# Row sums moved to ScalarE, the spread of the roots moved three steps on, and four smaller moves in a transformer layer on one core

## The chip, the cores and the metric

The kernel runs on one core of one Trainium2 chip. The metric is the device time of one execution in microseconds (us). Five engines work side by side: TensorE (PE in the profile; its weight loads are PEld), VectorE (DVE), ScalarE (ACT), GpSimd (POOL) and SyncE (SP), which issues most DMAs here. Each engine takes its instructions strictly in the order in which they were laid down for it.

## What is computed

The input x has 4 sequences of 1024 tokens with 256 channels. All numbers are float32. The reference adds two blocks to x, each with a layer norm ahead of it:

```python
x = x + attention(layernorm(x))      # RWKV: 16 heads of 16 channels
x = x + experts(layernorm(x))        # 8 experts, two for each token, at most 320 rows each
...
def layernorm(x):
    m, v = mean(x), var(x)           # over the 256 channels
    return (x - m) / sqrt(v + 1e-5)
...
# attention, per head, in chunks of tokens
att = rc @ kc
yc = att * Wmat @ vc + rc @ state * wb
new_state = ws * state + kc * wk @ vc
# then each head's y is normed, scaled, shifted, multiplied by gelu(xg @ Wg.T), and sent through Wo
...
# experts: softmax and top two of 8 logits, then for each expert on its rows
out = (silu(x @ w1) * (x @ w3)) @ w2
```

## The kernel before: tiles, stages and order

**Tiles.** The 4096 tokens are 16 blocks of 256 tokens (`TB`), four to a sequence. A block is two tiles of 128 tokens. Norms are taken for 512 tokens (`RT` = 4 tiles) at a time, apart from the very first 512 tokens, whose two halves are normed one after the other (`n` = 2).

**One attention block** is made of three generators. Each `yield` in them is a seam at which the order may pass to other work.

- `front` (L350) makes the block's inputs. Its steps are: the normed rows `xn` (ACT); their transposes `trx` on PE, the copy `xT` (ACT) and the shift difference `xx` (POOL, L379); the mix `xm` for the keys (DVE, L385); the keys `pc` on PE (L395) with the copy `kT`; the receptance `rT`, `rbT` and the mix for the gate `xm_g` (POOL); the values `pt` (L432); the transposed keys `pk` (L447) and `kw`; the gate `gT` (gelu on ACT, L458).
- `chunk` (L460), twice for a block: four score products `pa` (L470), multiplied by the decay `wmat` into `aw` (DVE, L478, four of 128x512); later the outputs `y` (L492, L499) and the state's update `pu` (L511) with `upd` (DVE, L518).
- `back` (L532) norms y by heads: squares and a copy on ACT; variances `pv` on PE (L547); a reciprocal root made of small DVE operations in two parts (`rsqrt`, L299: a first guess with one step, then a second step, ending in `ry`, L316); the spread of the roots to all channels `prs` on PE (L562); products `ys` and `zT` on DVE (L569, L570); the output product `po` on PE (L578) and its addition to x (L583).

**Norms.** `norm_stats` (L320) takes a `bn_stats` and a `bn_aggr` for each tile on DVE (L328, L329), then the root in about ten small DVE operations, and the shift `nb` (L336). It is called in three ways: for the two halves of the first 512 tokens, for the attention's next 512 tokens (`st` in the loop, 7 times), and for the experts' norm inside `logits` (8 times).

**Experts.** After 512 tokens are through the attention, `logits` and `route` (L589, L643) compute which experts they go to, and POOL scatters each row to DRAM, to a place of its expert (L783, 8 or 16 scatters). A job is one expert on the rows of one stretch `s`: SP loads weights and rows (`xe`, L831), PE transposes the rows (`pe`, L852), DVE copies them (`xeT`, L858), then come the products `p` (L883), silu on ACT (`sl`), the product `act` on DVE (L872), the results `pw` (L904) and an indirect DMA that adds them to the output (L911). A job of stretch s may begin only when `due(s)` holds: its routing lies at least `LAG` steps back (L948).

**The order of the work.** PE's order is written out by hand (`manual_schedule`, L1052): each block n runs a table of 15 steps (L1067 to L1083), and each step advances some generators. `f` is the front of block n+1, `fa` that of block n+2, `bk` the back of block n-1, `new` that of block n. After each step two seams of the routing are passed (`steps(routing, 2)`), and expert work follows as far as a credit of columns (`RATES`) allows. The other engines' orders are made by a planner, which follows the program's order and its own idea of when inputs are ready. `issue_after` ties an instruction behind another. PSUM has eight banks: tag "m" has four, "f" three and "y" one.

In the table before, `back` is stepped at these places of the next block: `pv` and the first root step at 3, the second root step at 4, `prs` and `zT` at 5, right behind `y` and `pu` of the first chunk, and `po` at 10.

Of the kernel before, what the change touches and what calls it, by code (L numbers as in the profile page):

```python
# [9 lines left out]
F32 = mybir.dt.float32  # L10
I32 = mybir.dt.int32
AF = mybir.ActivationFunctionType
ALU = mybir.AluOpType
# [4 lines left out]
P = 128  # L18
B, T, C = 4, 1024, 256
# [4 lines left out]
TB = 256  # L24
TPB = TB // P
BPS = T // TB
RB = 512
RT = RB // P
# [18 lines left out]
LN_EPS = 1e-5  # L47
# [5 lines left out]

RATES = (470, 1470, 1400, 1400)

LAG = 4

SCORES = (0, 6)
MAGIC = 0x5F3759DF
ROOT = (64.0 / 9.0) ** 2  # L60
# [3 lines left out]
def rwkv_then_moe_kernel(  # L64
# [12 lines left out]
    nc = tc.nc  # L77

    const = ctx.enter_context(tc.tile_pool(name="const", bufs=1))
# [3 lines left out]
    sm = ctx.enter_context(tc.tile_pool(name="sm", bufs=1))  # L83
# [5 lines left out]
    def bank(tag, name):  # L89
        return ps.tile(  # L90
            [P, 512], F32, tag=tag, name=name, bufs={"m": 4, "y": 1, "f": 3}[tag])
# [10 lines left out]
    xb = {}  # L102
# [5 lines left out]
    def load_x(b, r, step=RT):  # L108
        t = keep.tile([P, RT, C], F32, tag="x", name=f"x{b}_{r}", bufs=4)
        src = rows(x, b, r)  # L110
        for i in range(0, RT, step):
            nc.sync.dma_start(out=t[:, i:i + step, :], in_=src[:, i:i + step, :])
        xb[b, r] = t
# [26 lines left out]
    ones = const.tile([P, P], F32, tag="ones", name="ones")  # L140
# [87 lines left out]
    def decay_of_heads(cc):  # L228
        for i in range(cc * HC, (cc + 1) * HC):
            h = order[i]  # L230
            nc.scalar.activation(wmat[:, i, :], dist, AF.Exp, scale=nlam[:, h:h + 1])
# [67 lines left out]
    def rsqrt(v, n, nm):  # L299

        y = sm.tile([P, n], F32, tag=f"ry{n}", name=f"ry{nm}", bufs=2)
        a = sm.tile([P, n], F32, tag=f"ra{n}", name=f"ra{nm}", bufs=2)

        def guess():
            yi, vi, ai = y.bitcast(I32), v.bitcast(I32), a.bitcast(I32)
            nc.vector.tensor_tensor(ai, vi, one_i.to_broadcast([P, n]), ALU.logical_shift_right)
            nc.vector.tensor_tensor(yi, magic_i.to_broadcast([P, n]), ai, ALU.subtract)
            step(1.0)  # L310

        def step(scale):
            nc.vector.scalar_tensor_tensor(a, y, scale, y, ALU.mult, ALU.mult)
            nc.vector.tensor_tensor(a, a, v, ALU.mult)
            nc.vector.scalar_tensor_tensor(a, a, -10.0 / 3.0, a, ALU.add, ALU.mult)
            nc.vector.scalar_tensor_tensor(y, a, 5.0, y, ALU.add, ALU.mult)  # L316

        return y, (guess, lambda: step(9.0 / 64.0))

    def norm_stats(key, src, nm, t0=0, n=RT, behind=None):  # L320

        st = sm.tile([P, n, 6], F32, tag=f"st{n}", name=f"st{nm}", bufs=2)
        mv = sm.tile([P, n, 2], F32, tag=f"mv{n}", name=f"mv{nm}", bufs=2)
        ve = sm.tile([P, n], F32, tag=f"ve{n}", name=f"ve{nm}", bufs=2)
        nb = sm.tile([P, n], F32, tag=f"nb{n}", name=f"nb{nm}", bufs=2)
        for t in range(n):
            with tc.issue_after(behind) if behind else nullcontext():
                nc.vector.bn_stats(st[:, t, :], src[:, t0 + t, :])  # L328
            nc.vector.bn_aggr(mv[:, t, :], st[:, t, :])  # L329
            yield  # L330
        nc.vector.tensor_scalar(ve, mv[:, :, 1], LN_EPS, ROOT, ALU.add, ALU.mult)
        rs, parts = rsqrt(ve, n, nm)
        parts[0]()
        yield
        parts[1]()
        last["nb"] = nc.vector.scalar_tensor_tensor(  # L336
            nb, mv[:, :, 0], -1.0, rs, ALU.mult, ALU.mult).ins
        stats[key] = rs, nb, t0

    stats = {}  # L340

    def normed(dst, src, key, t):
        rs, nb, t0 = stats[key]
        t -= t0
        return nc.scalar.activation(
            dst, src, AF.Identity, bias=nb[:, t:t + 1], scale=rs[:, t:t + 1])

    last = {"base": None, "adds": []}

    def front(b, blk, o):  # L350

        nm = f"{b}_{blk}"
        r, h0 = divmod(blk * TPB, RT)
        src = xb[b, r]
# [9 lines left out]
        xT = a2.tile([P, CC, TB + 1], F32, tag="xT", name=f"xT{nm}")  # L364
# [6 lines left out]
        for cc in range(CC):  # L371
# [4 lines left out]
        last["xT_copy"] = nc.scalar.copy(  # L376
            xT[:, :, 1:TB + 1], pt.rearrange("p (cc i) -> p cc i", cc=CC)).ins
        xx = a1.tile([P, CC, TB], F32, tag="xx", name=f"xx{nm}")
        last["xx"] = last["pool"] = nc.gpsimd.tensor_tensor(  # L379
            xx, xT[:, :, 0:TB], xT[:, :, 1:TB + 1], ALU.subtract).ins  # L380

        def mixed(m):
            xm = a1.tile([P, CC, TB], F32, tag="xm", name=f"xm{nm}_{m}", bufs=3)
# [205 lines left out]
    def logits(b, r):  # L589

        nm = f"{b}_{r}"
        nc.sync.dma_start(out=rows(out, b, r), in_=xb[b, r])
        yield from norm_stats(("f", b, r), xb[b, r], f"f{nm}")
        yield
        hs = a2.tile([P, RT, W], F32, tag="hs", name=f"hs{nm}")
# [346 lines left out]
    clock = Block()  # L942
# [4 lines left out]

    def due(s):  # L948
        g = AFTER[s]
        return g in clock.routed and clock.step >= clock.routed[g] + LAG  # L950

    def flags(e):

# [30 lines left out]
    def routed(b, r):  # L984
        yield from logits(b, r)
        g = segment_of(b, r)
        if (r + 1) * RT == SEGMENTS[g][1] + SEGMENTS[g][2]:
            yield from route(g)
            clock.routed[g] = clock.step

    def steps(gen, n=1):
        for _ in range(n):
            next(gen, None)
# [3 lines left out]
    def fronts(n):  # L997
        if n >= NBLK:
            return iter(()), None
        b, blk = divmod(n, BPS)  # L1000
        o = Block()
        return front(b, blk, o), o
# [3 lines left out]

    for _ in norm_stats(("a", 0, 0, 0), xb[0, 0], "a0_0", 0, TPB):
        pass
    with tc.issue_after(last["nb"]):
        for _ in norm_stats(("a", 0, 0, 1), xb[0, 0], "a0_1", TPB, TPB):  # L1010
            pass
    f, cur = fronts(0)
    steps(f, 4)
    first_xm = last["xm"]
    with tc.issue_after(last["first_xn"]):
        decay_of_heads(0)
    with tc.issue_after(last["xT_copy"]):
# [33 lines left out]
    bk, routing, credit = iter(()), iter(()), 0  # L1051
    with tc.manual_schedule(engines={ENG.PE}):  # L1052
        for n in range(NBLK):
            b, blk = divmod(n, BPS)
            f, (fa, after) = f1, fronts(n + 2)
            st = iter(())
            if n + 2 < NBLK and n % RPS == 0:
                sb, sblk = divmod(n + 2, BPS)
                sr = sblk * TPB // RT
                st = norm_stats(("a", sb, sr, 0), xb[sb, sr], f"a{sb}_{sblk}", behind=last["xm"] if n else first_xm)  # L1060
            if blk % RPS == 0 and b + 1 < B:
                load_x(b + 1, blk // RPS)
            if blk == 0:
                last["state"] = None
            c = [chunk(b, blk, t, cur) for t in range(TPB)]
            new = back(b, blk, cur)
            for i, stage in enumerate((  # L1067
                (c[0], st),
                (f, st),
                (c[0], st),  # L1070
                (bk, st),
                (f, bk, st),
                (c[0], bk, st),
                (c[1], fa, st),
                (f,),
                (fa,),
                (c[1],),
                (bk,),
                (f,),
                (c[1], fa, new),  # L1080
                (f,),
                (bk,),
            )):  # L1083
                for part in stage:
                    steps(part)
                steps(routing, 2)
                clock.step += 1
                credit = min(credit + RATES[clock.turn], 4 * RATES[clock.turn])

                drain = i in SCORES  # L1090
                while credit > 0 or drain:
                    drain = False
                    cols = next(work, None)
                    if cols is None:
                        break
                    credit -= cols
            if n and n * TPB % RT == 0:
                pb, pblk = divmod(n - 1, BPS)
                routing = chain(routing, routed(pb, pblk * TPB // RT))
            cur, nxt, f1, bk = nxt, after, fa, new  # L1100

        clock.mixed = True
        for _ in chain(bk, routing, routed(B - 1, RPS - 1)):
            clock.step += 1
            if clock.step % 2:
                next(work, None)
        clock.mixed = False

        over = sm.tile([P, E + 1], F32, tag="over", name="over")
        nc.vector.tensor_scalar_add(  # L1110
            over[:, :E], last["base"], -float((TILES[B - 1] + SURE) * P))
        nc.vector.tensor_reduce(over[:, E:], last["base"], AX.X, ALU.max)
        nc.vector.tensor_scalar_add(over[:, E:], over[:, E:], -float(TILES[B] * P))
        last["over"] = sm.tile([P, E + 1], I32, tag="overi", name="overi")
        nc.vector.tensor_copy(last["over"], over)
        for _ in work:
            clock.step += 1
# [42 lines left out]
```

## Time and profile before

| | |
|---|---|
| median of 3 runs | 1009.61 us (1008.65 to 1011.55) |
| the profiled execution | 1007.76 us, its span 1006.0 us |
| PE busy | 944.5 us (94%) |
| PEld busy | 751.0 us (75%) |
| DVE busy | 471.6 us (47%) |
| ACT busy | 262.5 us (26%) |
| POOL busy | 247.4 us (25%) |

The span is the time from the first to the last instruction that the profile holds; 1.76 us of the execution's time lie around it. Busy time of an engine is the time that its instructions cover. The profile also cuts the span into 40 slices of 25.15 us with a busy share for each engine; in that table PEclk is the share of full clock that was granted to TensorE. A group of instructions is written as line, engine, operation, what is written and what is read, with the mean duration of one in ns and the idle time ahead of it, put down to whatever ended that idle time.

One product in the code is two MATMUL records in the profile, while a transpose is one: `front` has 3 x 4 key, receptance and gate products in each of 16 blocks, which is 192, and the groups of L395 hold 256 + 128 = 384 records.

### The profile page before, as it was taken

Reading aid. Unit: us, or ns where it says so; the run is one execution under the profiler, and the core shown is the slowest. Engines: PE = TensorE matmul, PEld = TensorE weight load, DVE = VectorE, ACT = ScalarE, POOL = GpSimd, SP = SyncE. Lnnn points to the kernel's source line nnn. Section 1 sums busy time; section 2 is a strip of 40 time slices with the busy share of each in tenths; the row PEclk is TensorE's granted clock in tenths of the full one; section 3 lists DMA queues with packets and bytes.
Section 4 is the critical chain, followed back from the end, with each engine's and each line's share of the span. In section 5 each row is a group of like instructions: output and inputs, shape, how many; then the busy total and the mean of one; then the engine's idle time right before and its main releaser. Section 6 shows DMA issues by size and latency. Waiting matters only on the chain. (4 is left out here: it accounts for less than half of the span.)

```text
span 1006.0 us, 16923 instructions
## 1 busy us (share of the span) xinstructions
PE 944.5 (94%) x6718; PEld 751.0 (75%) x6718; DVE 471.6 (47%) x1436; ACT 262.5 (26%) x559; POOL 247.4 (25%) x268
## 2 busy tenths in 40 slices
PE   5889889999999799999999899999999999999996
PEld 3666677878777678888888777888876866867764
DVE  7888746856677444454544344522222221222221
ACT  5324334244433323132221311311110111111110
POOL 6212410511125501212144111172111111211111
PEclk9999879999999999999999999999999999999998
DMA  5993133444424623334455445576654145423421
GB/s 171 273 302 129 49 129 97 168 131 134 161 88 156 202 79 127 101 114 128 132 164 169 140 117 163 153 222 212 178 164 119 39 142 147 127 56 123 148 53 19
DMA packets 92072, 139.05 MB, mean 138 GB/s; under 512 B 5456, under 2 KB 73552, under 8 KB 91984
## 3 DMA queue, kind: packets, MB, share of 16 engines
q1 hardware_dynamic: 79120, 120.36, 37.0%
q0 software_dynamic: 12720, 17.47, 9.1%
q8 instruction: 58, 0.95, 0.4%
q14 instruction: 30, 0.25, 0.1%
q10 hardware_dynamic: 144, 0.02, 0.0%
HBM read 103.45 MB, written 34.39 MB: 137 GB/s over the span
## 5 line engine op out<-in xcount | busy, mean ns | idle before, releaser
L883 PE MATMUL p<-xeT,w 128*128 128x256 f32 (+2 forms) x1960 | 436.2, 378 | 5.2 <-DVE xeT L858 3.9
L883 PEld LDWEIGHTS p<-xeT,w 128*128 128x128 f32 x1960 | 332.6, 195 | 95.3 <-issue 8.4
L872 DVE TENSOR_TENSOR act<-sl,p 128x256 f32<-128x256 f32 (+2 forms) x245 | 99.5, 408 | 281.9 <-ACT sl L888 166.0
L888 ACT ACTIVATE sl<-p 128x256 f32<-128x256 f32 (+2 forms) x245 | 91.0, 374 | 477.4 <-PE p L883 450.7
L904 PE MATMUL pw<-w,act 128*128 128x256 f32 x938 | 211.2, 381 | 0.5 <-DVE act L872 0.4
L911 POOL DMA_INDIRECT y_out<-ye,xe x67 | 104.6, 1561 | 434.9 <-DVE ye L908 358.5
L904 PEld LDWEIGHTS pw<-w,act 128*128 128x128 f32 x938 | 175.2, 190 | 25.8 <-issue 1.5
L908 DVE TENSOR_SCALAR ye<-pw,xe 128x256 f32<-128x256 f32 x67 | 32.1, 483 | 128.9 <-PE pw L904 128.9
L478 DVE TENSOR_TENSOR aw<-pa,wmat 128x512 f32<-128x512 f32 x128 | 79.4, 684 | 11.3 <-PE pa L470 11.1
L395 PE MATMUL pc<-xm,wa 128*128 128x256 f32 x256 | 66.8, 408 | 5.5 <-DVE xm L385 4.2
L783 POOL DMA_INDIRECT disp<-hs,is x64 | 63.7, 996 | 29.9 <-issue 15.9
L395 PEld LDWEIGHTS pc<-xm,wa 128*128 128x128 f32 x256 | 50.2, 204 | 16.8 <-DVE xm L385 5.8
L385 DVE SCALAR_TENSOR_TENSOR xm<-xx,ch,xT 128x256 f32<-128x256 f32 x96 | 43.9, 487 | 39.1 <-POOL xx L379 32.1
L470 PE MATMUL pa<-rT,kT 32*128 32x256 f32 x512 | 42.0, 412 | 4.1 <-ACT gT L458 3.4
L529 POOL TENSOR_TENSOR state<-state,upd 128x64 f32<-128x64 f32 x24 | 9.1, 377 | 139.5 <-DVE upd L518 125.7
L499 PE MATMUL y<-aw,vpad 128*32 128x128 f32 x1024 | 40.8, 278 | 0.2 <-DVE aw L478 0.2
L470 PEld LDWEIGHTS pa<-rT,kT 32*128 32x128 f32 x512 | 25.6, 188 | 14.3 <-ACT gT L458 5.0
L499 PEld LDWEIGHTS y<-aw,vpad 128*32 128x32 f32 x1024 | 24.5, 109 | 12.9 <-issue 11.3
L422 POOL TENSOR_TENSOR xm_g<-xx,ch 128x512 f32<-128x512 f32 x16 | 17.9, 1119 | 63.6 <-PE pc L395 63.5
L432 PE MATMUL pt<-wa,xm 128*128 128x256 f32 x128 | 32.3, 397 | 0.0
L395 PE MATMUL pc<-xm_g,wa 128*128 128x256 f32 x128 | 31.1, 385 | 0.3 <-POOL empty L1028 0.3
L578 PE MATMUL po<-wa,zT 128*128 128x256 f32 x128 | 30.3, 379 | 0.0
(174 smaller groups left out, 763.3 us busy)
## 6 DMA issues: line engine op xcount, KB each, us to landing
w<-w_in SPq DMA_DIRECT2D x96, 896.0 KB, 6.5
disp<-empty SPq DMA_DIRECT2D x8, 795.0 KB, 13.9
disp<-empty SPq DMA_DIRECT2D x16, 265.0 KB, 8.0
xe<-disp SPq DMA_DIRECT2D x16, 265.0 KB, 2.8
xe<-disp SPq DMA_DIRECT2D x8, 530.0 KB, 3.8
y_out<-x SPq DMA_DIRECT2D x8, 512.0 KB, 3.5
x<-x_in SPq DMA_DIRECT2D x7, 512.0 KB, 4.0
wa<-w_attn_in SPq DMA_DIRECT2D x5, 256.0 KB, 5.3
```

Source lines behind the costliest of these rows:

```text
L385: last["xm"] = nc.vector.scalar_tensor_tensor(xm[:, cc, :], xx[:, cc, :], maa(m, cc), xT[:, cc, 1:TB + 1], ALU.mult, ALU.add,).ins
L395: nc.tensor.matmul(pp[:, m * TB:(m + 1) * TB], wa[w][:, cc, m * P:(m + 1) * P], xm[:, cc, :], start=cc == 0, stop=cc == CC - 1,)
L432: nc.tensor.matmul(pv[:, t * C:(t + 1) * C], xm_v[:, cc, t * P:(t + 1) * P], wa[W_V][:, cc, :], start=cc == 0, stop=cc == CC - 1,)
L470: nc.tensor.matmul(pa[g][:, cc * TB:(cc + 1) * TB], o.kT[rows32, cc, cols], o.rT[rows32, cc, :, cols], start=True, stop=True, tile_positio ...
L478: nc.vector.tensor_tensor(w.rearrange("p q i -> p (q i)"), pa[g], wmat[:, 4 * g:4 * g + 4, :].rearrange("p q i -> p (q i)"), ALU.mult,)
L499: nc.tensor.matmul(y[32 * g:32 * g + 32, :], o.vp[:, t, cc * 4 + g, q * 32:(q + 1) * 32], aw[g][:, cc * 2 + q, :], start=state is None and ...
L783: ins = nc.gpsimd.indirect_dma_start(out=disp[:, :], out_offset=bass.IndirectOffsetOnAxis(ap=idx_s[g][:, c, t:t + 1], axis=0), in_=last["h ...
L872: nc.vector.tensor_tensor(act, sl, p3[:, :w], ALU.mult)
L883: nc.tensor.matmul(pp[:, :w], wt[:, cc, f * P:(f + 1) * P], xeT[:, cc, lo:lo + w], start=cc == 0, stop=cc == CC - 1,)
L888: nc.scalar.activation(sl, p1[:, :w], AF.Silu)
L904: nc.tensor.matmul(po[:, :C], acts[f][:, i * P:(i + 1) * P], w2e[:, f, :], start=f == 0, stop=f == FC - 1,)
L911: ins = nc.gpsimd.indirect_dma_start(out=out[:, :], out_offset=bass.IndirectOffsetOnAxis(ap=xe.bitcast(I32)[:, t, C:C + 1], axis=0), in_=y ...
```

## The change

1. `norm_stats` with four tiles takes the sums on ScalarE: a Copy scaled by -1/256 with an accumulator (minus the mean), then a Square with that mean as bias and an accumulator (256 times the variance). With two tiles it stays on VectorE. 15 calls of four tiles are changed.
2. `prs` and `zT` move from step 5 to step 8, `po` from 10 to 11, and the transposed keys `pk` from 11 to 10.
3. PE runs 20 products of a 128x128 tile of ones ahead of everything; nothing reads their result.
4. The shift difference `xx` of the very first block is taken by VectorE and no longer by GpSimd.
5. `LAG` = 4 for all stretches becomes `LAGS` = (8, 5, 4, 4).
6. The second half of the first 512 tokens' norm is traced after the first four steps of the first front, with its last root step behind the first mix products.

```diff
-LAG = 4
+LAGS = (8, 5, 4, 4)
+WARM = 20
...
     def norm_stats(key, src, nm, t0=0, n=RT, behind=None):
-        for t in range(n):
-            with tc.issue_after(behind) if behind else nullcontext():
-                nc.vector.bn_stats(st[:, t, :], src[:, t0 + t, :])
-            nc.vector.bn_aggr(mv[:, t, :], st[:, t, :])
-            yield
-        nc.vector.tensor_scalar(ve, mv[:, :, 1], LN_EPS, ROOT, ALU.add, ALU.mult)
+        if n < RT:
...
+        else:
+            mean, sign = sm.tile([P, n], F32, tag="mn", name=f"mn{nm}", bufs=2), 1.0
+            for t in range(n):
+                with tc.issue_after(behind) if behind else nullcontext():
+                    nc.scalar.activation(
+                        aside, src[:, t0 + t, :], AF.Copy, scale=-1.0 / C,
+                        accum_out=mean[:, t:t + 1])
+                nc.scalar.activation(
+                    aside, src[:, t0 + t, :], AF.Square, bias=mean[:, t:t + 1],
+                    accum_out=ve[:, t:t + 1])
+                yield
+            nc.vector.tensor_scalar(ve, ve, ROOT / C, LN_EPS * ROOT, ALU.mult, ALU.add)
...
-        last["xx"] = last["pool"] = nc.gpsimd.tensor_tensor(
-            xx, xT[:, :, 0:TB], xT[:, :, 1:TB + 1], ALU.subtract).ins
+        if b == 0 and blk == 0:
+            nc.vector.tensor_tensor(xx, xT[:, :, 0:TB], xT[:, :, 1:TB + 1], ALU.subtract)
+        else:
+            last["pool"] = nc.gpsimd.tensor_tensor(
+                xx, xT[:, :, 0:TB], xT[:, :, 1:TB + 1], ALU.subtract).ins
...
-        return g in clock.routed and clock.step >= clock.routed[g] + LAG
+        return g in clock.routed and clock.step >= clock.routed[g] + LAGS[s]
...
-    with tc.issue_after(last["nb"]):
-        for _ in norm_stats(("a", 0, 0, 1), xb[0, 0], "a0_1", TPB, TPB):
-            pass
+    first_nb = last["nb"]
+
+    warm = bank("f", "warm")
+    for _ in range(WARM):
+        nc.tensor.matmul(warm[:, :P], ones, ones, start=True, stop=True)
     f, cur = fronts(0)
     steps(f, 4)
     first_xm = last["xm"]
+
+    second = norm_stats(("a", 0, 0, 1), xb[0, 0], "a0_1", TPB, TPB)
+    with tc.issue_after(first_nb):
+        steps(second, TPB + 1)
+    with tc.issue_after(first_xm):
+        steps(second)
...
                 (bk, st),
                 (f, bk, st),
-                (c[0], bk, st),
+                (c[0], st),
                 (c[1], fa, st),
                 (f,),
-                (fa,),
+                (fa, bk),
                 (c[1],),
+                (f,),
                 (bk,),
-                (f,),
                 (c[1], fa, new),
                 (f,),
-                (bk,),
+                (),
```

More of the change, by code (lines that the diff above doesn't have):

```diff
@@ L320, in norm_stats @@
     def norm_stats(key, src, nm, t0=0, n=RT, behind=None):
-        st = sm.tile([P, n, 6], F32, tag=f"st{n}", name=f"st{nm}", bufs=2)
-        mv = sm.tile([P, n, 2], F32, tag=f"mv{n}", name=f"mv{nm}", bufs=2)
         ve = sm.tile([P, n], F32, tag=f"ve{n}", name=f"ve{nm}", bufs=2)
         nb = sm.tile([P, n], F32, tag=f"nb{n}", name=f"nb{nm}", bufs=2)
-        for t in range(n):
-            with tc.issue_after(behind) if behind else nullcontext():
+        if n < RT:
+            st = sm.tile([P, n, 6], F32, tag="st", name=f"st{nm}", bufs=2)
+            mv = sm.tile([P, n, 2], F32, tag="mv", name=f"mv{nm}", bufs=2)
+            for t in range(n):
                 nc.vector.bn_stats(st[:, t, :], src[:, t0 + t, :])
-            nc.vector.bn_aggr(mv[:, t, :], st[:, t, :])
-            yield
-        nc.vector.tensor_scalar(ve, mv[:, :, 1], LN_EPS, ROOT, ALU.add, ALU.mult)
+                nc.vector.bn_aggr(mv[:, t, :], st[:, t, :])
+                yield
+            mean, sign = mv[:, :, 0], -1.0
+            nc.vector.tensor_scalar(ve, mv[:, :, 1], LN_EPS, ROOT, ALU.add, ALU.mult)
+        else:
+            mean, sign = sm.tile([P, n], F32, tag="mn", name=f"mn{nm}", bufs=2), 1.0
+            for t in range(n):
+                with tc.issue_after(behind) if behind else nullcontext():
[5 more added lines that the diff above has]
+                    accum_out=ve[:, t:t + 1])
+                yield
+            nc.vector.tensor_scalar(ve, ve, ROOT / C, LN_EPS * ROOT, ALU.mult, ALU.add)
         rs, parts = rsqrt(ve, n, nm)
@@ L336, in norm_stats @@
         last["nb"] = nc.vector.scalar_tensor_tensor(
-            nb, mv[:, :, 0], -1.0, rs, ALU.mult, ALU.mult).ins
+            nb, mean, sign, rs, ALU.mult, ALU.mult).ins
         stats[key] = rs, nb, t0
     stats = {}
+    aside = const.tile([P, C], F32, tag="aside", name="aside")
     def normed(dst, src, key, t):
```

## The prediction

> **What bounds the kernel now.** I read the page's slices first, then the stages, then what PE waited for in each, then the two longest waits in order of time.
>
> ```profile
> PE   5889889999999799999999899999999999999996
> DVE  7888746856677444454544344522222221222221
> PEclk9999879999999999999999999999999999999998
> ```
>
> PE is full from slice 15 (377 us) on, so nothing is to be had there. It is not full in the first 100 to 150 us, and DVE is as busy as PE there. The stages (busy us and instructions of PE, PEld, DVE, ACT, POOL, granted clock, DMA share, GB/s):
>
> ```profile
> 0.00:26.80 26.80, 13.92 (x60) 9.82 (x60) 20.04 (x74) 15.05 (x38) 16.83 (x39) 1.00 0.57 176
> 26.80:113.80 87.00, 74.70 (x941) 55.65 (x942) 76.21 (x259) 31.39 (x62) 20.77 (x28) 1.00 0.73 201
> 113.80:137.30 23.50, 18.23 (x143) 14.97 (x144) 11.13 (x35) 8.10 (x18) 8.19 (x11) 0.65 0.23 75
> 137.30:355.00 217.70, 203.62 (x2000) 168.25 (x2000) 141.14 (x473) 83.92 (x172) 65.04 (x75) 0.98 0.44 143
> ```
>
> From 26.8 to 113.8 us DVE (76.2) is busier than PE (74.7), with ACT at 31.4: the four blocks without expert work are bound by DVE. What PE waited for from 26.8 to 137.3 us (total, times, longest):
>
> ```profile
> PE prs L562 <- DVE upd L518: 6.3, 3, 2.9
> PE pe L852 <- DMA xe<-disp: 4.8, 1, 4.8
> PE prs L562 <- DVE ryh L316: 4.3, 1, 4.3
> PE pc L395 <- DVE xm L385: 1.8, 1, 1.8
> PE trx L373 <- ACT xn L345: 1.1, 2, 0.9
> ```
>
> The root's spread waits once in each of blocks 1 to 4: 6.3 + 4.3 = 10.6 us. PE's timeline around the two longest waits (start, length, line, what, idle ahead):
>
> ```profile
> 109.16 0.31 PE L511 MATMUL pu<-vpad,kw 128*32 128x32 f32 x16
> 113.80 1.23 PE L562 MATMUL prs<-ryh,spread 64*128 64x128 f32 x8 [4.34 <-DVE ryh L316]
> 114.96 2.09 PE L470 MATMUL pa<-rT,kT 32*128 32x256 f32 x16
> ...
> 124.83 0.31 PE L511 MATMUL pu<-vpad,kw 128*32 128x32 f32 x16
> 129.89 0.69 PE L852 MATMUL pe<-ident,xe 128*128 128x128 f32 x2 [4.75 <-DMA xe<-disp]
> 131.09 6.78 PE L883 MATMUL p<-xeT,w 128*128 128x128 f32 x32 [0.52 <-DVE xeT L858]
> ```
>
> Each is paid twice: scores `pa` take 2.09 us after the first wait where they take 1.15 elsewhere. The granted clock is 0.50 from 113.4 to 120.2 (PE busy 6.4 us, half of it lost: 3.2) and from 127.1 to 137.3 (busy 6.9, lost 3.4).
>
> **The parts of the change.**
>
> *a. Start.* 20 products are 40 records. The first 16 records of `pc` take 6.76 us at 12.03, the next such 16 take 3.72 at 26.80: the start runs at half clock, which the clock column does not show. Cold, a record of 128 columns is half of 6.76/16, so 0.21 us, and 40 take 8.5 us; warm from halfway, some 6.5. `ones` is ready at 1.15 and the first transposes start at 8.28, so they cost from nothing to 1.4 us. The gain is up to 3.0 us on `pc`. `xx` on DVE is not in the trace; the nearest rows for 512 columns are a copy at 0.60 and a subtraction at 0.68 against 1.04 on POOL, so 0.4 us earlier. But DVE runs without a break from 11.5 to 24 us (mixes, centred values, nine and seven diagonals), and `xx` (0.68) and the second norm's last five operations (1.0) are put into it. PE's next wait, 1.79 at 26.80, is for the second block's `xx`, which POOL starts at 25.19 behind memsets and selects, and POOL's `xm_g` ahead of those waits for `pc`. I take 2 us; ends: 1.5 lost, 4.3 won.
>
> *b. Blocks 0 to 3.* Off DVE go, per tile:
>
> ```profile
> L328 DVE BATCH_NORM_STATS2 sta<-x 128x6 f32<-128x256 f32 x32 | 12.7, 415 | 2.8 <-DMA x<-x_in 2.8
> L329 DVE BATCH_NORM_AGGREGATE mva<-sta 128x2 f32<-128x6 f32 x32 | 5.3, 173 | 0.0
> L345 ACT ACTIVATE xn<-x,nba,rya 128x256 f32<-128x256 f32 x32 | 18.2, 602 | 25.7 <-DVE nba L336 25.7
> L437 ACT COPY vpad<-pt 128x256 f32<-128x256 f32 x32 | 10.3, 374 | 54.9 <-PE pt L432 54.9
> ```
>
> That is 0.59 us, for 60 tiles 35 us in all; from 26.8 to 113.8, 18 tiles or 10.3 us by the same two rows. ACT gets two operations per tile. Accumulating ones are not in the trace; the nearest rows of 256 columns are 0.37 and 0.60, so 0.75 to 1.2 us, in all 45 to 72 us, and double if each accumulator costs another short instruction (0.2, as a copy of 2 columns). ACT has 262 busy of 1006 and 31 of 87 in this stage; that idle time hides it. Uncovered, a norm is 4 x 1.2 = 4.8 us ahead of `kT` or `gT` in ACT's queue.
>
> The Trainium skill speaks against this: ScalarE: Activation LUTs, Rules for kernel authors, gives adds and multiplies to VectorE. The rows agree per tile (0.59 on DVE, 0.75 or more on ACT); by that alone the 60 tiles would cost 10 us or more, but only if ACT were the late engine, which no wait of this stage shows. Its section What ACT_TABLE_LOAD costs would give, as an estimate, 0.40 for the Copy and 0.49 for the Square.
>
> The spread moved to step 8 has the second chunk's `pa` (1.15), `pt` (1.9) and `trx` (0.6) ahead of it, 3.6 us more cover than the waits of 1.41, 2.92 and 1.95 in blocks 1 to 3 need. With 0.95 at `trx` in block 0, whose norm leaves DVE, 7.2 us go. What is late next is `po`: it needs `zT`, which ends 1.54 us after the spread (two `ys`, two `zT`, 71.38 to 72.92), and at step 11 only `pk` (0.60) lies between. That is 1.0 us in each of three blocks. If the four `aw` (2.48) stand ahead of `ys` on DVE it is 3.5. Net 4.2 won; ends: 7.2 won, 3.2 lost.
>
> *c. Block 4 and the first job.* From the routing's count on PE (ended 106.05) to `pe` (129.89) 23.8 us pass. The chain: DVE to the row numbers 4.5; scatters on POOL, 8 x 1.27, with `xx` (1.04) and a state step (0.3), 13.3 with its 1.54 wait for PE's late `trx`, so 11.5 without it; landing and load, 5.6. That is 21.6 without the wait. PE's own work in the stretch is 12.8 at full clock. `LAGS[0]` puts four steps more ahead of `pe`: 13 (`pc` 1.9), 14 (nothing), 0 (`pa` 1.15) and 1 (`pc` 1.9), 4.9 in all. So 17.7 plus 1.0 for `po` stand against 21.6: a wait of 2.9 stays, with one half-clock stretch (1.7 lost for 3.4). Won: 23.8 - 21.6 + 4.9 = 7.2, and 1.7 of clock: 8.9. Ends: the chain stays at 23.8, 4.9; all is covered, 11.0 + 3.4 = 14.4.
>
> *d. From 137 us on.* Waits at `prs` come to 1.0 + 0.7 + 0.8. Expert work at steps 8 to 10 covers `zT` there. The wait at 343.5 for stretch 1 (3.5 us) has one step more, step 2, which holds no PE work: nothing. Waits of `pa` for `gT` (3.4) may grow with ACT's load, those for `aw` shrink with DVE's. I take 1 us; ends: 6 won, 5 lost. Later stretches only pass work from one time to another.
>
> **Sum.** 2 + 4.2 + 8.9 + 1 = 16.1 us. The profiled execution took 1007.76, so 991.7; it lies 1.85 under the median of the runs, so a median of 993.5.
>
> **Rivals.**
>
> 1. *PE only runs into the next wait.* DVE's relief lets PE reach `pe` sooner, the chain stays at 23.8 and the half clock as it was (c gives 4.9), and `po` waits its full 3.5 in blocks 1 to 3 (b gives -3.2). Sum 2 + 4.9 - 3.2 + 1 = 4.7: 1005. For it: one wait in the traces is always followed by the next one. Against: the `po` group had no idle time ahead of it so far. Chance 0.15, with anything from 1000 to 1006.5.
> 2. *Slower: `po` takes over the wait.* Place: step 11 of blocks 1 to 4, where no expert work lies between `prs` and `po`. If DVE runs as late there as it did at 113.80 (4.3 us), `po` waits 0.95 + 4.3 = 5.2, four times 21, with a half-clock stretch each (4 x 1.7 = 7). Against the 2 + 7.2 + 8.9 won, that is +10: a median of 1020. It decides from a lag of some 3.6 us. For it: root, `aw` and mixes still share DVE. Against: 10.3 us leave DVE. Chance 0.10.
> 3. *ACT becomes the late engine.* One us behind ACT's queue for each of the 15 norms eats the gain: 1008, no change. Chance 0.05.
> 4. *The clock falls again before the first `pc`.* PE idles 2.4 us between `trx` and `pc`. At 127.1 the clock fell 2.0 us into a wait that began at 125.13. Then a gives nothing: 995.5. The Trainium skill, TensorE: Matmul & The Clock Gate, Part 1, lets it fall only after an idle window of 3.4 us, by which the warming would hold; the trace's 2.0 us is against it. Chance 0.15, inside the forecast's range.
> 5. *More than the sum*: the lighter DVE also shortens the 13.5 us of waits from 137 to 355. 980. Chance 0.10.
>
> **Numbers.** The forecast, without or with 4, has 0.60 (985 to 1000); rival 1 has 0.15, 2 0.10, 3 0.05, 5 0.10. A measurement here can tell 0.3% (3 us) from no change. Faster: 0.60 + 0.15 + 0.10 = 0.85; same 0.05; slower 0.10. The range takes in rivals 1 and most of 5 and the ends of a to c: 981 to 1007.
>
> **What would show it.** Right: no idle time ahead of `prs` before 114 us, no half clock there, `po` waits of about 1 us, a wait at the first `pe` under 4 us, ACT near 320 to 340 busy, DVE near 437. Wrong: `po` waits of over 3 us, `pa` waiting for `gT` in every block, or transposes that start after 10 us.

## The result and the profile after

The changed kernel took 996.66 us (median of 4 runs, 996.37 to 998.01) against 1009.13 (1007.96 to 1011.55): a ratio of 0.987 [0.9842, 0.9898], 12.5 us less where 16.1 were forecast, and 3.2 us from the predicted median. Its profiled execution took 998.01, the longest of the four, with a span of 996.3: 9.75 less than the profiled execution before, which with 1007.76 was shorter than each of the four runs of its kernel. All step sizes below are of these two executions, so they add up to 9.8 and not to 12.5.

The page's slices (25 us each now) of the kernel after:

```profile
PE   7999899999999899999999998999999999999995
DVE  7888766676576543544543434422222222222221
ACT  5637445644654423243413222311110111101110
PEclk9999989999999999999999998999999999999998
```

PE is fuller in the first ten slices. The clock column still dips in the slice at 125 us and once more at 600. DVE looks no lighter. The same stages as before (busy us of PE, PEld, DVE, ACT, POOL, then clock, DMA share, GB/s):

```profile
0.00:26.80 26.80, 19.51 (x102) 16.42 (x103) 20.38 (x76) 15.94 (x45) 15.85 (x38) 0.94 0.67 208
26.80:113.80 87.00, 80.50 (x982) 59.24 (x981) 76.22 (x231) 50.99 (x135) 23.69 (x31) 1.00 0.70 196
113.80:137.30 23.50, 20.26 (x167) 15.42 (x167) 13.70 (x50) 13.28 (x39) 7.30 (x10) 0.85 0.25 80
137.30:355.00 217.70, 207.06 (x2084) 168.85 (x2083) 136.92 (x432) 107.00 (x269) 62.80 (x74) 0.99 0.43 141
```

In the second row PE went from 74.70 to 80.50 and ACT from 31.39 to 50.99, but DVE, which the prediction wanted relieved, is at 76.22 after 76.21: the blocks pass faster (982 records of PE instead of 941), and more of DVE's other work falls into the same 87 us. PE's waits from 26.8 to 137.3 us:

```profile
PE po L599 <- DVE zT L591: 2.7, 2, 1.6
PE pa L491 <- ACT gT L479: 2.4, 1, 2.4
PE pt L453 <- DVE rbT L436: 1.2, 1, 1.2
PE po L599 <- ACT xn L363: 1.0, 1, 1.0
```

`prs` and `pe` are gone from this list; `po` came in (three waits, 3.7 us), and `pa`, `pt`. PE's timeline around block 4 and the first job:

```profile
110.47 0.93 PE L583 MATMUL prs<-ryh,spread 64*128 64x128 f32 x8
111.33 0.66 PE L468 MATMUL pk<-ident,kT 128*128 128x128 f32 x4
113.63 1.97 PE L599 MATMUL po<-wa,zT 128*128 128x256 f32 x8 [1.64 <-DVE zT L591]
...
119.42 1.34 PE L491 MATMUL pa<-rT,kT 32*128 32x256 f32 x6
123.19 2.07 PE L491 MATMUL pa<-rT,kT 32*128 32x256 f32 x10 [2.43 <-ACT gT L479]
125.55 3.78 PE L416 MATMUL pc<-xm,wa 128*128 128x256 f32 x8 [0.29 <-DVE aw L499]
129.12 0.63 PE L873 MATMUL pe<-ident,xe 128*128 128x128 f32 x2
```

The spread runs without a wait, its product `po` waits 1.64, and `pe` finds its tokens there. But the scores wait 2.43 for the gate `gT`, and the mix products behind them take 3.78 where they take 1.99 at full clock: from 123.1 to 130.0 the clock is 0.51 with PE busy 6.27, 3.1 us lost. The scores do not read `gT`. By the code they are written into the four PSUM banks of tag "m", and the gate's product holds one of these until the gelu has read it.

Why `gT` was late stands in ACT's timeline of the same kernel:

```profile
119.52 0.42 ACT L340 ACTIVATE aside<-x 128x256 f32<-128x256 f32 x1 [7.18 <-DVE x L604]
119.84 0.19 ACT L340 ACTIVATION_READ_ACCUMULATOR aside<-x 128x1 f32 x1
...
120.57 0.58 ACT L558 ACTIVATE sq<-y 128x512 f32<-128x512 f32 x1
...
122.56 0.57 ACT L479 ACTIVATE gT<-pc 128x512 f32<-128x512 f32 x1
```

The norm's first Copy stood at the head of ACT's queue for 7.18 us, waiting for `x` with `po` added (DVE, L604). The squares `sq` and the gate were behind it, and three more sums came ahead of the gate.

Where the time went can be followed in PE's timelines, since from the 21st expert job on both kernels run the same order:

| point on PE | before | after | gained |
|---|---|---|---|
| first `pc` of the second block (block 1) | 26.80 | 26.40 | 0.4 |
| block 3's second `y` | 98.84 | 96.48 | 2.4 |
| first job's `pe` | 129.89 | 129.12 | 0.8, and 4.5 of step work more ahead of it |
| second job's `pe` | 145.12 | 141.10 | 4.0, and 4.1 of step work more ahead of it |
| 21st job's `pe` | 660.45 | 650.68 | 9.8 |
| last job's `pe` | 958.11 | 948.34 | 9.8 |

Blocks are counted from 0, as in the prediction. The step work comes from `LAGS[0]` and is added up from the start of one row to the start of the next: for the first job the products `pc`, `pa` and `pc` of the steps that go ahead of it (1.73 + 1.08 + 1.73; the prediction had 4.9 from lengths of rows, which overlap), for the second a `pv`, a `pc` and a group of `y` and `pu` (0.36 + 1.73 + 1.98).

### The profile page after: what moved, and what is told of

Read it like the earlier page. It is cut to its first block, busy times and chain, and to the rows that moved or that the text cites. A ratio compares the mean times of both kernels' runs of the same rounds, so it can differ in the third digit from the quotient of the medians.

```text
span 996.3 us, 17100 instructions
## 1 busy us (share of the span) xinstructions
PE 950.4 (95%) x6758; PEld 752.5 (76%) x6758; DVE 458.1 (46%) x1317; ACT 319.4 (32%) x797; POOL 246.5 (25%) x267
## 5 line engine op out<-in xcount | busy, mean ns | idle before, releaser
L904 PE MATMUL p<-xeT,w 128*128 128x256 f32 (+2 forms) x1960 | 431.8, 374 | 5.0 <-DVE xeT L879 3.8
L904 PEld LDWEIGHTS p<-xeT,w 128*128 128x128 f32 x1960 | 327.2, 191 | 95.1 <-issue 9.2
L925 PE MATMUL pw<-w,act 128*128 128x256 f32 x938 | 214.4, 384 | 1.2 <-DVE act L893 1.1
L416 PE MATMUL pc<-xm,wa 128*128 128x256 f32 x256 | 63.7, 394 | 3.2 <-DVE xm L406 1.9
L416 PEld LDWEIGHTS pc<-xm,wa 128*128 128x128 f32 x256 | 47.8, 194 | 13.9 <-DVE xm L406 3.5
L491 PE MATMUL pa<-rT,kT 32*128 32x256 f32 x512 | 44.2, 410 | 6.2 <-ACT gT L479 5.9
L340 ACT ACTIVATE aside<-x 128x256 f32<-128x256 f32 x60 | 24.9, 415 | 51.8 <-DVE x L604 51.0
```

The source lines that it names most:

```text
L416: nc.tensor.matmul(pp[:, m * TB:(m + 1) * TB], wa[w][:, cc, m * P:(m + 1) * P], xm[:, cc, :], start=cc == 0, stop=cc == CC - 1,)
L491: nc.tensor.matmul(pa[g][:, cc * TB:(cc + 1) * TB], o.kT[rows32, cc, cols], o.rT[rows32, cc, :, cols], start=True, stop=True, tile_positio ...
L904: nc.tensor.matmul(pp[:, :w], wt[:, cc, f * P:(f + 1) * P], xeT[:, cc, lo:lo + w], start=cc == 0, stop=cc == CC - 1,)
L925: nc.tensor.matmul(po[:, :C], acts[f][:, i * P:(i + 1) * P], w2e[:, f, :], start=f == 0, stop=f == FC - 1,)
```

## The experiments

Two theories stood against each other. **Order**: the gain is the new table, since `prs` has other products ahead of it while the root is computed. **Relief**: the gain is the 10.3 us that leave DVE. The first four runs undo or do one of the two (before: 1014.9 us on their chip).

**One half at a time.** Undone sums (not shown: buffers of their own for four tiles, and the tie `behind` for `bn_stats`):

```diff
-        if n < RT:
+        if n <= RT:
...
```

> The changed kernel with all norm sums back on VectorE (bn_stats and bn_aggr); everything else stays changed. Theory 'relief': the waits at the root's spread came from VectorE's load, so the 35 us of sums come back to it and most of the gain goes: 1004 to 1008 us, with the po waits of blocks 1, 2 and 4 (1.0, 1.1, 1.6 us) growing to 2 to 4 us each. Theory 'order': the waits came from where the table put the spread, the sums on ScalarE are worth little and even cost the 2.4 us wait of the scores for gT at 120.8 us with the half clock behind it: 993 to 998 us, and that wait is gone.

Measured: 1001.78 us, 0.9889 [0.9851, 0.9927]. The wait of the scores for `gT` is gone from 26.8 to 137.3 us: the gelu, at 123.17, waits only for its product (0.94 us). The waits at `po` did not grow as relief had it (3.3 us in three waits, 3.7 in the change).

Undone table:

```diff
-                (c[0], st),
+                (c[0], bk, st),
...
-                (fa, bk),
+                (fa,),
...
-                (f,),
                 (bk,),
+                (f,),
...
-                (),
+                (bk,),
```

> The changed kernel with the table of steps of before (spread at step 5, po at 10, pk at 11); everything else stays changed. Theory 'relief': VectorE, lighter by 35 us, has the roots ready, the waits at the spread stay small (under 1 us each in blocks 1 to 4): 995 to 999 us. Theory 'order': the spread waits again in blocks 1 to 4, 1.4 to 4.3 us each as before, and po waits are gone: 1002 to 1007 us.

Measured: 1011.58 us, 0.9973 [0.9952, 0.9994]. The old waits are back, from 26.8 to 137.3 us:

```profile
PE prs L583 <- DVE upd L539: 6.4, 3, 3.3
...
PE prs L583 <- DVE ryh L318: 3.1, 1, 3.1
```

Only the sums (the kernel before with the `else` branch of `norm_stats` from the diff):

> The kernel before with only the norm sums of four tiles moved to ScalarE. Theory 'relief': most of the gain comes with it: 998 to 1003 us, waits at the spread from 10.6 us down to under 4 in blocks 1 to 4. Theory 'order': 1006 to 1010 us, waits at the spread stay near 10 us.

Measured: 1013.77 us, 0.9996 [0.9974, 1.0019]. Its stage of blocks 0 to 3, and its waits from 26.8 to 137.3 us:

```profile
26.80:113.80 87.00, 79.19 (x941) 58.73 (x941) 70.45 (x215) 47.68 (x127) 18.58 (x27) 0.94 0.78 200
```

```profile
PE prs L578 <- DVE upd L534: 6.6, 3, 3.3
PE pe L868 <- DMA xe<-disp: 5.1, 1, 5.1
PE prs L578 <- DVE ryh L316: 3.1, 1, 3.1
```

DVE was relieved here (76.21 to 70.45, ACT 31.39 to 47.68), and `prs` still waits 9.7 us of the former 10.6. The same 941 records of PE took 79.19 us here and 74.70 before, since the clock fell twice in this execution (0.94 in the mean); the ratio, from 12 runs, does not rest on that.

Only the table (the kernel before with the table's rows of the diff):

> The kernel before with only the new table of steps (spread at 8, po at 11, pk at 10). Theory 'relief': VectorE is as late as before, so the wait moves to po, 2 to 5 us in each of blocks 1 to 4: 1006 to 1012 us. Theory 'order': the 10.6 us at the spread go, po waits 1 us each: 1000 to 1004 us.

Measured: 1001.06 us, 0.9875 [0.9845, 0.9905], with no wait at `prs` and, from 26.8 to 137.3 us:

```profile
PE pe L852 <- DMA xe<-disp: 5.1, 1, 5.1
PE trx L373 <- ACT xn L345: 2.3, 4, 1.5
...
PE po L578 <- DVE zT L570: 1.4, 1, 1.4
PE po L578 <- issue: 1.3, 2, 1.0
```

All four agree. With the table and without the sums the gain is 1.1 and 1.2%; with the sums and without the table it is 0.3% (beside start and lag) and nothing. **Order holds, and relief falls.** The table's three moves (`prs` with `zT`, `po`, `pk`) were not undone one by one; two runs further down shift the first and the second. What relief overlooked stands in DVE's timeline of the kernel before, ahead of the longest wait at `prs`:

```profile
104.79 0.18 DVE L329 BATCH_NORM_AGGREGATE mvf<-stf 128x2 f32<-128x6 f32 x1
104.88 2.46 DVE L478 TENSOR_TENSOR aw<-pa,wmat 128x512 f32<-128x512 f32 x4
...
108.93 0.28 DVE L552 TENSOR_SCALAR var<-pv 128x128 f32<-128x128 f32 x1
...
111.58 0.29 DVE L316 SCALAR_TENSOR_TENSOR ryh<-rah,ryh 128x128 f32<-128x128 f32 x1
111.79 0.68 DVE L415 TENSOR_TENSOR rbT<-pc,wb 128x512 f32<-128x512 f32 x1
...
113.37 0.29 DVE L316 SCALAR_TENSOR_TENSOR ryh<-rah,ryh 128x128 f32<-128x128 f32 x1
```

The last operation of a norm's sums ends at 104.97. From `var` at 108.93 to the end of the root at 113.66 there are 4.7 us of root steps, each needing the one before it, with routing steps and `rbT` among them, and no `bn_stats` at all. What left DVE had not stood in this wait. At most it had stood ahead of the chain: the four `aw` start 1.1 us after the scores `pa` end (103.76 to 104.88). In `only_sums` this wait is 1.27 shorter (3.07), and those in blocks 1 to 3 are not (6.6 against 6.3).

**The start alone** (the kernel before with the warm products, the first `xx` on DVE and the second norm later):

```diff
+    warm = bank("f", "warm")
+    for _ in range(WARM):
+        nc.tensor.matmul(warm[:, :P], ones, ones, start=True, stop=True)
...
+        if b == 0 and blk == 0:
+            nc.vector.tensor_tensor(xx, xT[:, :, 0:TB], xT[:, :, 1:TB + 1], ALU.subtract)
...
```

> The kernel before with the three edits of the start alone: 20 unused products, the first shift on VectorE, the second half's norm traced later. Prediction's term a: 2 us faster, a ratio of 0.998. Theory 'VectorE's queue': what PE gains at the first products it loses where it next waits for VectorE (centred value weights, mixes of the second block), and the clock falls there: between 1 us faster and 2 us slower, a ratio of 0.999 to 1.002.

Measured: 1009.49 us, 1.0005 [0.9987, 1.0024]: nothing. In this execution the clock fell in the 1.92 us ahead of the first `pc`, whose 16 records took 5.33; and the second block's wait grew from 1.79 to 3.67:

```profile
27.41 3.81 PE L399 MATMUL pc<-xm,wa 128*128 128x256 f32 x10 [3.67 <-DVE xm L389]
```

**The lag alone**, undone and done:

```diff
-LAGS = (8, 5, 4, 4)
+LAGS = (4, 4, 4, 4)
```

> The changed kernel with four steps ahead of every stretch's turn again (8, 5, 4, 4 back to 4, 4, 4, 4). Theory 'cover': the four steps more hold 4.9 us of PE work that covers the rows of the first job; without them PE waits 4 to 7 us at the first pe and the clock falls there: 4 to 6 us slower than the changed kernel, a ratio to before of 0.991 to 0.993. Theory 'moved': with the steps the wait only turned into the one of the scores for gT (2.4 us) with the same half clock, so undoing it changes less than 2 us: a ratio of 0.986 to 0.989.

Measured: 1000.27 us, 0.9915 [0.9889, 0.9941], with the wait back:

```profile
PE pe L873 <- DMA xe<-disp: 5.2, 1, 5.2
```

Here the loads are issued at 120.8 (before: 126.1), and the first `pe` runs at 122.92, 7.0 us earlier than before with the same work ahead of it. Of these, 2.3 us were there when the routing's count began on PE (103.26, before 105.52).

> The kernel before with the new table of steps and the new LAGS, nothing else. The table alone gave a ratio of 0.9875 with a 5.1 us wait at the first pe. Theory 'cover': that wait goes, 4 to 7 us more: a ratio of 0.981 to 0.984, better than the whole change. Theory 'moved': another wait takes its place: 0.986 to 0.989.

Measured (the kernel before with the table and `LAGS`): 997.7 us, 0.9894 [0.9868, 0.992], beside 0.9875 [0.9845, 0.9905] for the table alone. The wait at `pe` is gone, and `pc` waits 2.28 for `aw` at 122 us in its place. The lag's own worth is not shown: its three pairs (0.987 or 0.9881 against 0.9915; 0.9894 against 0.9875; 0.9831 against 0.9824 below) differ in sign, and all their intervals overlap.

**The gate ahead of the norm.** To take away the 2.43 us at `pa`, the experts' norm was put behind the gate in ACT's queue:

```diff
-        nc.scalar.activation(o.gT, channel_major(W_G, xm_g), AF.Gelu)
+        last["gT"] = nc.scalar.activation(o.gT, channel_major(W_G, xm_g), AF.Gelu).ins
...
-        yield from norm_stats(("f", b, r), xb[b, r], f"f{nm}")
+        yield from norm_stats(("f", b, r), xb[b, r], f"f{nm}", behind=last["gT"])
```

> The changed kernel, with the sums of the experts' norms queued behind the gate's gelu on ScalarE (so that gT no longer stands behind a sum that waits for x). Theory 'blocked queue': the 2.4 us wait of the scores for gT near 120 us and the half clock after it (some 3 us) go, and the other waits for gT (3.5 us from 137 to 355) shrink: 3 to 6 us faster than the changed kernel, a ratio of 0.981 to 0.984. Theory 'chain': x itself is late, the wait passes to the norm's end and to hs: under 1 us, a ratio of 0.986 to 0.988.

Measured: 1002.09 us, 0.9933 [0.9907, 0.9959]: a miss, outside both theories and 5.4 us longer than the change's 996.66 (0.987). The waits for `gT` did go (none up to 137.3 us, 0.5 after it up to 355), and others came. PE's waits, from 137.3 to 355 us and, in the second fence, from 26.8 to 137.3:

```profile
PE trh L637 <- ACT hs L363: 4.5, 4, 2.6
```

```profile
PE plt L658 <- ACT lgT L655: 2.9, 1, 2.9
```

The norm itself is now late, and with it `hs`, its transposes and the routing's logits. Here the wait at `gT` was the price of the experts' norm being early.

**The cover of `po`.** The prediction named `po` as late next. Here `po` goes one step on, behind the scan's `y` and `pu` (the kernel before with the table and this):

```diff
-                (bk,),
-                (c[1], fa, new),
+                (),
+                (c[1], bk, fa, new),
```

> The kernel before with the new table, but the output product po one step later still, at step 12 behind y and pu of the second chunk. With the new table alone PE waited for zT at po 1.0 to 1.5 us in blocks 1, 2 and 4 and 2.2 us at 221 us. Theory 'order' (a wait is the cover that the table lacks): y and pu put 1.9 us more ahead, the po waits go, 3 to 6 us faster than the table alone, a ratio of 0.981 to 0.985. Theory 'passed on': x is added later, and the next norm and y wait for it or for kw: within 2 us of the table alone, 0.986 to 0.990.

Measured: **991.71 us**, 0.9824 [0.9797, 0.9852], as expected; the interval just overlaps that of the table alone, 0.9875 [0.9845, 0.9905], on another chip. From 26.8 to 137.3 us `po` waits no more, and `pe` still does:

```profile
PE pe L852 <- DMA xe<-disp: 6.1, 1, 6.1
PE trx L373 <- ACT xn L345: 2.8, 4, 1.5
```

The change itself, run again beside it on the same chip:

> The changed kernel once more, beside these three on one chip: a ratio of 0.984 to 0.990 if it is worth what the table alone is.

Measured: 997.77 us (995.27 to 1000.89), 0.9881 [0.9852, 0.9909]. `po_later` ran from 990.88 to 994.04, below every run of the change, and it has neither the sums on ACT nor the start nor `LAGS`. No version of this study has a lower median. With `LAGS` as well:

> As po_later, with LAGS (8, 5, 4, 4) too. Theory 'order': both waits go, po's and the 5 us at the first pe: a ratio of 0.977 to 0.983, the fastest of all. Theory 'passed on': 0.986 to 0.990.

Measured: 992.2 us, 0.9831 [0.9804, 0.9858], no different from `po_later` and just outside what order gave. The 6.1 at `pe` is gone, and this came in its place, from 26.8 to 137.3 us:

```profile
PE pc L395 <- DVE aw L478: 2.8, 1, 2.8
```

**How far the spread has to move** (the kernel before with the table, but `prs` and `zT` at step 7):

```diff
-                (f,),
-                (fa, bk),
+                (f, bk),
+                (fa,),
```

> The kernel before with the new table, but the spread and zT one step earlier, at step 7 behind the values pt, po still at 11. The spread then has 3.05 us more cover than in the table before, po has trx (0.6) and pk (0.6) ahead of it. Theory 'order': waits at the spread stay under 0.5 us in blocks 1 to 3 and about 1.3 in block 4 (4.34 less 3.05), po waits shrink by 0.6 each: within 2 us of the table alone, a ratio of 0.984 to 0.989. Theory 'relief' (VectorE is late as a whole): the spread waits 1.5 us or more in each block: 0.990 to 0.995.

Measured: 997.29 us, 0.9865 [0.9835, 0.9895]. Blocks 1 to 3 have no wait at `prs` and block 4 one of 1.4, as expected; `po` was expected to wait less and waits 3.5:

```profile
PE po L578 <- DVE zT L570: 3.5, 2, 1.8
...
PE prs L562 <- ACT xn L345: 1.4, 1, 1.4
```

So step 7 is as good as step 8 as far as these runs can tell: the root's delay needs the second chunk's `pa` and `pt`, and hardly the step after them.

## Why the prediction was right, and where it was wrong

| term | predicted | measured | from |
|---|---|---|---|
| a start | 2 | 0.4 | second block's first `pc` |
| b blocks 0 to 3 | 4.2 | 2.0 | block 3's second `y`, 2.4 less 0.4 |
| c block 4, first job | 8.9 | 5.7 | second job's `pe`, 4.0 + 4.1 less 2.4 |
| d the rest | 1 | 1.7 | 9.8 less the others |
| sum | 16.1 | 9.8 | |

The direction and the place held, and the median within 3.2 us: the waits at `prs` went, `po` came next with about 1 us a block, and most of the gain is made before 150 us. Three terms were too large, and one reason was wrong.

**a was mis-sized.** The part that was worked out came: the first `pc` takes 3.72 instead of 6.76, and the warm products delay nothing that shows. But the time was not kept. The lines of the start:

```profile
1.20 7.52 PE L1034 MATMUL warm<-ones 128*128 128x128 f32 x40 [1.20 <-POOL ones L143]
...
11.36 3.72 PE L416 MATMUL pc<-xm,wa 128*128 128x256 f32 x16 [1.92 <-DVE xm L406]
17.91 3.38 PE L453 MATMUL pt<-wa,xm 128*128 128x256 f32 x8 [2.83 <-DVE wa L206]
```

The chunk's next product, `pt`, waits 2.83 us for the centred weights, which stand in DVE's queue behind the mixes, and then runs at half clock (0.50 from 17.3 to 20.7; 3.38 instead of 1.89). In `change_again` and `only_start` it went the other way: the clock fell ahead of the first `pc` (5.41 and 5.33), and PE waited 3.59 and 3.67 at the second block's `pc`, which began at 27.42 and 27.41, 0.6 later than before. Its mixes need `xx` from POOL, and there POOL starts it at 25.81 and 25.80, behind its memsets and selects; before it was 25.19. The prediction named this wait for `xx` and the full queue of DVE, and priced only what is put in, not that PE would come to both sooner. `only_start` agrees: nothing won.

**b was right in mechanism for the table, wrong in its reason.** "The four blocks without expert work are bound by DVE" failed: `only_sums` took 5.8 us of DVE's busy time out of this stage and won nothing measurable. The gain goes with the prediction's other reason, that `prs` has 3.6 us more work ahead of it. In size, the waits at `prs` and `trx` went as said, and `po` took less than its price of 1.0 in each of three blocks: 1.00 and 1.05 in blocks 1 and 2, none in block 3 (the 1.64 is block 4's and falls under c). What the prediction had put at nothing were 1.2 at `pt`, behind `rbT`, and 0.4 more at each of `y` and `plt`. Up to block 3's second `y` PE's idle time fell by 3.1 us (8.0 to 4.9), and its busy time for the same work rose by 1.1 (64.1 to 65.2), for which no run gives the cause; that leaves 2.0 instead of 4.2. The sums cost what was said on ACT: 0.415 for the Copy and 0.507 for the Square and, as the prediction's last clause allowed, a separate instruction for each accumulator:

```profile
L340 ACT ACTIVATE aside<-x 128x256 f32<-128x256 f32 x60 | 24.9, 415 | 51.8 <-DVE x L604 51.0
```

```profile
L340 ACT ACTIVATION_READ_ACCUMULATOR aside<-x 128x1 f32 x60 | 11.3, 189 | 0.0
```

That is 0.415 + 0.507 + 2 x 0.19 = 1.30 us a tile by the rows; they overlap, and ACT's busy time went from 262.5 to 319.4 (320 to 340 said), 0.95 a tile. DVE's went only to 458.1 (437 said; 457.1 in `only_sums`): 35 us of durations left, but the rows overlap and some of those that stayed became longer, and how much each does is not settled. The 51.0 us in the first line are ACT's idle time in front of this Copy, 14 times.

**c was mis-sized: the chain gave more than said, and PE's own way to the first job took it back.** From the end of the routing's count to `pe`, 23.8 us became 19.1 in `undo_lags`, where PE still waits for the tokens; the prediction had 21.6. (Its 21.6 leaves out the gaps between the rows: 23.8 less the wait of 1.5 is 22.3, which would have made c 8.2.) "A wait of 2.9 stays" failed: PE arrives 6 us after the tokens, an estimate from the loads' issue at 120.5 and the 2.1 us that `undo_lags` shows from there to `pe`. The prediction gave PE 18.7 us for its own way, `po` included; from the count's end at 103.7 to `pe` at 129.1 it took 25.4. In it are the wait of `pa` for `gT`, 2.43, which had been put at nothing here, and the half-clock stretch that follows, 3.1, for which 1.7 had been counted. That is rival 3's mechanism, ACT late, at one place instead of 15; that `gT` would be the one to wait for was said under "Wrong". `undo_sums` shows the cause: with the sums back on DVE this wait is gone, and the second job's `pe` comes at 138.76 (141.10 in the change).

**d** was nearly right as a net (1.7 for 1), not in its parts: the waits from 137.3 to 355 us fell from 14.1 (13.5 in the prediction) to 10.6, the one of 3.5 at stretch 1's first load went, and a new one came, with the clock at half from 604.4 to 611.2:

```profile
605.62 1.23 PE L583 MATMUL prs<-ryh,spread 64*128 64x128 f32 x8 [3.86 <-DVE ryh L318]
```

What caused this one was not tried.

**Of the rivals**, 1 came in part: a wait in the place of almost each that went, but at 12 us less in all (PE's waits after 26.8 us: 40.4 before, 28.4 after). Rival 2 did not come; `po` lagged 1.6 at most, under its point of 3.6. Rival 4 came in some executions and not in others: after a wait of 1.92 or 1.93 us the first `pc` took 3.72 in one execution of the changed kernel and 5.41 in the other (`change_again`). The Trainium skill (TensorE: Matmul & The Clock Gate, Part 1) lets the clock fall only after an idle window of about 3.4 us; these falls came after shorter ones, so here the trace does not agree with it as it stands.

Open are the worth of `LAGS`, and what the sums are worth beside the table: undone they give 0.9889 [0.9851, 0.9927], no different from the change. Up to 137.3 us PE's waits show both sides: without the sums `trx` waits 1.7 us instead of 0.3, with them `pa` waits 2.4 for `gT`.

## What to carry to other kernels

A stage in which an engine is the busiest is not thereby bound by it: read which instructions stand between the last thing that came and the wait, and take away or cover those; work removed elsewhere in the queue bought nothing here. A wait on a chain of small dependent steps was covered here by reordering the waiting engine's own independent work, and then once more for the next consumer: covering `po` too gave 0.9824 where the table alone gave 0.9875 and the whole change, on the same chip, 0.9881. A sum put into an in-order queue brings its own input's wait with it: what counts is what stands behind it, not the free time of the engine.

## What the runs showed of the hardware

The clock fell after waits that look harmless. In `only_table` a wait of 1.52 us at 109.75 (PE busy 1.72 of the 3.4 us from 109.3) is followed by 0.50 from 112.7 on; in the kernel before, a wait of 2.92 at 67.7 was followed by no fall at all. Inside the run the half-clock stretches last 3.4 us or two or three times that (17.3 to 20.7; 123.1 to 130.0 and 604.4 to 611.2; 127.1 to 137.3 in the kernel before). Whether a given wait costs such a stretch differs between executions of one kernel, as the first `pc` showed (3.72 or 5.41, 1.7 us). Single runs of the same kernel differ by several us, and the longer ones have the lower clock: `only_table` ran from 999.93 us with a mean granted clock of 0.988 to 1005.38 with 0.981. So the sizes above, from single executions, are good to a few us only.
